# A second quad's rows loaded singly, by two engines, in a graph-attention kernel

## The chip, the cores and the metric

The kernel runs on one core of a Trainium2 chip. The metric is the device time of one execution in microseconds, from repeated runs; beside it stands one execution with the hardware profiler. Engines: PE (TensorE, matmuls; PEld is its weight loads), DVE (VectorE), ACT (ScalarE), POOL (GpSimd) and SP (SyncE). ACTq, SPq and POOLq are the queues of instructions of those engines that issue DMAs, load registers and wait.

## The reference

One layer of graph attention with 12,500 nodes, 200,000 edges sorted by target, 4 heads of 32:

```python
h = jnp.maximum(_layernorm(x, axis=-1), 0.0)
h = (node_features @ W_node.T).reshape(num_nodes, H, HD)
e = (edge_features @ W_edge.T).reshape(num_edges, H, HD)
h_src = h[src]
h_tgt = h[tgt]
att = jnp.sum(jnp.concatenate([h_src, h_tgt, e], axis=-1) * a, axis=-1)
att = jnp.where(att > 0, att, 0.2 * att)
m = jnp.maximum(jax.ops.segment_max(att, tgt, num_segments=num_nodes), 0.0)
ex = jnp.exp(att - m[tgt])
denom = jax.ops.segment_sum(ex, tgt, ...) + (num_edges - deg)[:, None] * jnp.exp(-m)
h_prime = jax.ops.segment_sum((ex / denom[tgt])[:, :, None] * h_src, tgt, ...)
x = x + h_prime
```

So each edge needs the row of its source node (h and the attention term of the source), found by an index that is known only as data.

## The kernel before, in words

Edges are cut into 392 groups of 512 (511 and a place for what is carried over); four groups are a quad, 98 quads in all, numbered from 0. A group is 4 chunks of 128 edges, so a quad has 16 chunks of 128 edges, one edge per partition.

First the node rows are made (layer norm, product with W_node) and written to a table in DRAM, 137 floats or 548 bytes a row: the four heads, counts and the source's attention terms. Then, quad by quad, POOL gathers the source rows with one indirect DMA for each chunk (128 rows, `gather`, L185) into one of eight places of the tile `ga` (quad number modulo 8). The gathers of the first quads read x itself, before the table is there.

Quads pass through three stages, which alternate in the order in which the code issues them:

- *Logits* (`all_logits`): VectorE marks each edge's target (`at`), PE multiplies edge features and target terms into `lg`, ACT copies that to `tg`. `add_sources` ends the stage: ACT waits for the quad's gathers by a semaphore that counts them, and copies the source terms out of `ga` into `U` (L798).
- *Softmax* over a super, a set of mostly four quads (`softmax`): transposes of U on PE, then VectorE and ACT in turn (`low`, scans for the running maxima, `fac`, `stack` with the exponentials, `xs`).
- *Sums* (`sums(q)`): one step for each of the quad's four groups; VectorE weighs the gathered rows and makes the one-hot `hot`, PE multiplies them into `acc`. Then the sums are passed on and divided (`passed_on` with ACT's `den_of` and VectorE's `pt`, `divide_ranges`), and ACT prepares the next quad's `hot` and `ga` columns.

While sums(q) is issued, the logits of a later quad are, and behind the logits of the last quad of a super its softmax. Supers of four start at quads 7, 11, 15 and so on, so quad 48 is the second of its super (47 to 50), and quad 42 the last of 39 to 42. Each engine takes its instructions in program order. Windows of nodes are of four kinds (`CLASSES`), and change at quads 22, 36 and 75.

One quad, the 85th (`SINGLE = 84`, counted from 0), is not gathered by POOL. Its rows are loaded one by one: behind each sums step from quad 11 on (`SINGLES_FROM`), `single_rows` issues eight (`AT_A_STEP`) DMAs of one row each on SP's queue, into a part of the tile `db` that is free by then. The row's address comes from a register: SP fetches the 128 source numbers of a chunk (`fetch_places`), VectorE scales them to byte offsets (`scale_places`), and SP loads 16 of them at a time into registers (TENSOR_LOAD). 16 chunks x 16 steps are 256 steps, the sums of quads 11 to 74. Two semaphores, one for each half, count the landings; `add_sources(84)` waits for both.

SP also issues everything else that is loaded and stored in this phase: edge features `ea`, target numbers `db`, target terms `pw`, node inputs and results.

Of the kernel before, what the change touches and what calls it, by code (L numbers as in the profile page):

```python
# [9 lines left out]
F32 = mybir.dt.float32  # L10
# [7 lines left out]
P = 128  # L18
# [21 lines left out]
QUADS = 8  # L40
# [14 lines left out]
def blocks(total, step):  # L55
    return [(i, min(step, total - i)) for i in range(0, total, step)]
# [14 lines left out]
def kernel(  # L71
# [39 lines left out]
    nc = tc.nc  # L111
    NT = -(-(N + P) // P)
    NP = NT * P
# [8 lines left out]
    table = dram.tile([NP, ROW], F32, name="table")  # L122
# [33 lines left out]
    quads = blocks(G, QG)  # L156
# [13 lines left out]
    single_came = [tc.alloc_semaphore(f"single{k}") for k in range(2)]  # L170
    landings = {}

    def gather(q, rows, width, lo, hi):

        if q == SINGLE:
            return
        g0, m = quads[q]
        ga = GA[q] = ga_all[:, q % QUADS]
        chunks = lambda i: -(-min(E - (g0 + i) * NE + 1, GE) // P)
        for i in range(lo, hi):  # L180
            if chunks(i) < J:
                nc.vector.memset(ga[:, i, chunks(i):, :], 0.0)
        order = [(i, j) for i in range(lo, hi) for j in range(chunks(i))]
        for i, j in order:
            came = nc.gpsimd.indirect_dma_start(  # L185
                out=ga[:, i, j, 0:width], out_offset=None, in_=rows,
                in_offset=bass.IndirectOffsetOnAxis(ap=srci[:, g0 + i, j:j + 1], axis=0))
# [32 lines left out]
    with tc.manual_schedule():  # L220
# [25 lines left out]
        for _ in range(AT_ONCE):  # L246
            q, i = early.pop(0)
            gather(q, x, D, i, i + 1)
# [150 lines left out]
        with tc.tile_pool(name="node", bufs=2) as node, tc.tile_pool(  # L399
# [116 lines left out]
            step, steps = 0, sum(-(-T // 3) for T in sizes) - 9  # L516
            for b, (t0, T) in enumerate(sets):
# [5 lines left out]
                row = node.tile([P, NODE_T, ROW], F32, name="row")  # L523
# [24 lines left out]
    with tc.tile_pool(name="work", bufs=2) as work, \  # L548
# [86 lines left out]
        def fetch(q):  # L635
            if q not in EA:
                due["features"] += fetch_features(q)
            fetch_windows(q)
            if q not in GATHERED:
                GATHERED.add(q)  # L640
                gather(q, table, ROW, raws(q), quads[q][1])

        def fetch_rows(s):
            g0, m = groups(s)
            dr = DR[s] = turned.tile([SBG * H, NE + 2], I32, name="dr", bufs=2)
            if finer(s) > 1:
# [8 lines left out]
        n_own = QG * J * ROW  # L655
        GA[SINGLE] = own[:, QG * GE // 2:QG * GE // 2 + n_own].bitcast(F32).rearrange(
            "p (g j r) -> p g j r", g=QG, j=J)
        places = [own[0:1, QG * GE // 2 + n_own + k * P:QG * GE // 2 + n_own + (k + 1) * P]
                  for k in range(2)]
        single = {"step": 0, "landings": 0}  # L660
        steps = -(-P // AT_A_STEP)

        def fetch_places(n):

            if n >= QG * J:
                return
            g, j = quads[SINGLE][0] + n // J, n % J
            at = ((g // 2 * J + j) * 2 + g % 2) * P
            nc.sync.dma_start(places[n % 2], src[at:at + P].unsqueeze(0))

        def scale_places(n):

            if n < QG * J:
                nc.vector.tensor_scalar(places[n % 2], places[n % 2], float(4 * ROW), None,
                                        op0=OP.mult)

        def single_rows():

            if not single["step"]:
                fetch_places(0)  # L680
                scale_places(0)
            n, at = divmod(single["step"], steps)
            if n >= QG * J:
                return
            single["step"] += 1
            if not at:
                fetch_places(n + 1)
            if at == steps // 2:
                scale_places(n + 1)
            lo = at * AT_A_STEP  # L690
            if at % 2 == 0:
                single["values"] = nc.values_load_multi_w_load_instructions(
                    places[n % 2][:, lo:lo + 2 * AT_A_STEP], engines=[mybir.EngineType.SP],
                    min_val=0, max_val=(NP - 1) * 4 * ROW,
                    skip_runtime_bounds_check_because="a node's row")[1]
            for p in range(lo, lo + AT_A_STEP):
                came = nc.sync.dma_start(
                    as_bytes(GA[SINGLE][p:p + 1, n // J, n % J, :]),
                    rows_at(table, single["values"][p - at // 2 * 2 * AT_A_STEP], 4 * ROW, 1))
                came.then_inc(single_came[2 * n // (QG * J)], 16)  # L700
                tc.no_tile_sem_insts.add(came.ins.name)
                tc.add_to_no_dep_group(f"rows{SINGLE}", came.ins)
                single["landings"] += 16

        def open_logits(q):
            if q == supers[of_quad[q]][0]:
# [47 lines left out]
        def keep_logits(q):  # L754

            pair, half, full, n = place_of(q)
            if full and q in LG:
                tg = turned.tile([PAIR * KH, GE], F32, name="tg")
                TG[of_quad[q]] = tg, n, pair
                nc.scalar.copy(tg[:n], LG.pop(q)[:n])  # L760
# [18 lines left out]
        def add_sources(q):  # L779

            s = of_quad[q]
            g0, m = quads[q]
            s0, sm = groups(s)
            keep_logits(q)
            if s not in U:
                U[s] = turned.tile([P, J, SBG * H], F32, name="U", bufs=2)
            f = finer(s)
            u = U[s][:, 0:J // f, 0:sm * H * f].rearrange("p c (h w) -> p w c h", h=H)[
                :, (g0 - s0) * f:(g0 - s0 + m) * f]
            if q == SINGLE:  # L790
                assert single["landings"] == 16 * P * QG * J
                for came in single_came:
                    nc.scalar.wait_ge(came, single["landings"] // 2)
            elif q >= QUADS:
                nc.scalar.wait_ge(arrived[q % len(arrived)],
                                  sum(landings[a] for a in range(QUADS, q + 1) if a != SINGLE
                                      and a % len(arrived) == q % len(arrived)))
            taken = nc.scalar.copy(u, GA[q][:, :m].rearrange("p g (f c) r -> p (g f) c r", f=f)[  # L798
                :, :, :, R_SRC:R_SRC + H])
# [325 lines left out]
        def sums(q):  # L1125
# [36 lines left out]
            for i in range(m):  # L1162
# [36 lines left out]
                if q >= SINGLES_FROM:  # L1199
                    single_rows()  # L1200
# [291 lines left out]
        def flush():  # L1492

            if "logits" in state:
                add_sources(state.pop("logits"))
# [441 lines left out]
```

## Time and profile before

| | us |
|---|---|
| median of 3 runs (lowest to highest) | 1971.07 (1969.68 to 1973.94) |
| profiled execution | 1973.07 |
| its span | 1971.2 |
| busy: POOL, DVE, PE, ACT | 1477.5, 1193.8, 1134.6, 318.1 |
| POOL's gathers from the table, first and last start | 93.6, 1944.0 |
| SP's single rows, first and last start | 327.8, 1601.7 |
| granted TensorE clock, mean | 0.739 of full speed |

The span runs from the first to the last instruction of the profiled execution; the rest of its time lies around it. "Busy" leaves out what queues do: an ACT or SP that issues DMAs or loads registers counts as idle. "Idle before" in a row is the time in which that engine did nothing just before the instruction, with the one that ended it.

### The profile page before, as it was taken

The page shows a single profiled execution, that of the slowest core. Times are in us where ns is not written, and L with a number is a line of the kernel's source. Part 1 is how long each engine was busy: PE and PEld are TensorE (multiplying, and loading weights), DVE is VectorE, ACT ScalarE, POOL GpSimd, SP SyncE. Part 2 cuts the span into 40 slices and gives each one's busy share as a digit, 9 for nine tenths or more (in the row PEclk, how much of TensorE's full clock was granted, in tenths as well). Part 3 has the DMA queues.
Part 4 walks back from the last instruction along what each step waited for, and adds up shares of the span by engine and source line. Part 5 has one row for each costly group of instructions (what it writes and reads, how often), then busy time and mean ns, then how long its engine had stood idle before and what let it go on. Part 6 is the DMA issues. An engine that isn't in the chain of part 4 may idle for free.

```text
span 1971.2 us, 23138 instructions
## 1 busy us (share of the span) xinstructions
PE 1134.6 (58%) x5116; PEld 771.6 (39%) x5116; DVE 1193.8 (61%) x2631; ACT 318.1 (16%) x1077; POOL 1477.5 (75%) x1569
## 2 busy tenths in 40 slices
PE   6666676454555554646556555555464755555565
PEld 4544444333333342434334333344242433334344
DVE  8676887365464663746546546466374663767576
ACT  6664111001010010100000101001011011212122
POOL 7777777777777777777777777777777777777775
PEclk9788788676776766767767677777676766877678
DMA  7754754434444444444444444444444444544442
GB/s 257 209 134 100 177 135 107 106 93 107 103 106 107 102 113 102 117 101 118 104 119 103 114 108 113 110 112 110 113 109 99 105 122 109 128 114 116 98 107 56
DMA packets 171399, 229.87 MB, mean 117 GB/s; under 512 B 62636, under 2 KB 104542, under 8 KB 171255
## 3 DMA queue, kind: packets, MB, share of 16 engines
q0 software_dynamic: 49600, 108.49, 24.5%
q1 hardware_dynamic: 119952, 117.28, 21.0%
q10 hardware_dynamic: 1702, 2.59, 0.4%
q14 instruction: 104, 0.84, 0.1%
q8 instruction: 41, 0.67, 0.1%
HBM read 210.75 MB, written 17.43 MB: 116 GB/s over the span
## 4 chain that ended last, share of the span: by engine, by line
POOL 29%; DVE 27%; PE 15%; issue 13%; DMA 9%; ACT 5%; SPq 2%; ACTq 0%; POOLq 0%; DVEq 0%
POOL ga L185 29%; DMA ga<-table,srci 6%; PE acc L1186 6%; DVE at L717 4%; PE t_ps L855 2%; PE lg L747 2%; DVE ga L1112 2%; DVE t_ps L869 1%; DVE t_ps L868 1%; DVE t_ps L935 1%; DVE t_ps L932 1%; PE lg L750 1%; DVE pt L1019 1%; DVE hot L1095 1%; PE ex_ps L950 1%
## 5 line engine op out<-in xcount | busy, mean ns | idle before, releaser
L185 POOL DMA_INDIRECT ga<-table,srci x1478 | 1399.8, 947 | 451.8 <-issue 408.9
L1186 PE MATMUL acc<-ga,hot 128*113 128x137 f32 (+1 forms) x2904 | 536.3, 344 | 83.9 <-DVE hot L1095 43.4
L1186 PEld LDWEIGHTS acc<-ga,hot 128*113 128x113 f32 (+1 forms) x2904 | 476.5, 214 | 183.8 <-issue 78.9
L1019 DVE SCALAR_TENSOR_TENSOR pt<-pt,spare,acc 1x133 f32<-1x133 f32 x113 | 38.3, 339 | 484.4 <-ACT den_of L1013 483.0
L750 PE MATMUL lg<-at,pw 112*96 112x512 bf16 (+2 forms) x392 | 155.8, 434 | 266.6 <-DVE at L717 239.4
L717 DVE TENSOR_TENSOR at<-const_ps,db 112x1024 bf16<-112x1024 f32 (+1 forms) x176 | 212.9, 1211 | 43.4 <-DMA db<-offset 41.6
L747 PE MATMUL lg<-ea,by_pair 128*96 128x512 f32 (+1 forms) x392 | 229.5, 671 | 7.1 <-ACT tg L760 7.1
L1153 DVE TENSOR_TENSOR ga<-ga,ex_ps 128x1056 f32<-128x1056 f32 x145 | 179.7, 1240 | 0.0
L855 PE MATMUL t_ps<-ident,U 128*64 128x128 f32 (+2 forms) x210 | 46.4, 391 | 216.6 <-ACT U L798 216.6
L798 ACT COPY U<-ga 128x64 f32<-128x64 f32 x97 | 28.7, 297 | 786.7 <-DMA ga<-table,srci 786.7
L1155 DVE TENSOR_TENSOR hot<-const_ps,slot 128x896 f32<-128x896 f32 (+1 forms) x147 | 144.2, 981 | 0.0
L855 PEld LDWEIGHTS t_ps<-ident,U 128*64 128x64 f32 (+2 forms) x210 | 36.5, 198 | 242.8 <-ACT U L798 239.5
L950 PE MATMUL ex_ps<-ident,stack 128*128 128x128 f32 x105 | 28.5, 423 | 173.0 <-DVE stack L942 162.3
L750 PEld LDWEIGHTS <-pw 112*96 112x96 bf16 (+2 forms) x392 | 54.3, 139 | 103.3 <-issue 97.8
L1038 PEld LDWEIGHTS acc<-pt,spare 1*2 1x2 f32 x226 | 14.0, 86 | 204.2 <-issue 195.4
L950 PEld LDWEIGHTS ex_ps<-ident,stack 128*128 128x128 f32 x105 | 18.5, 214 | 186.9 <-ACT stack L940 186.9
L1112 DVE TENSOR_TENSOR ga<-ga,ex_ps 128x528 f32<-128x528 f32 x92 | 63.6, 693 | 37.3 <-ACT xs L956 37.2
L185 POOL DMA_INDIRECT ga<-in_x_dram,srci x72 | 68.5, 951 | 23.3 <-issue 18.9
L760 ACT COPY tg<-lg 96x512 f32<-96x512 f32 (+1 forms) x51 | 29.5, 579 | 297.4 <-PE lg L750 297.4
L776 PE MATMUL t_ps<-tg,of_head 96*64 96x512 f32 (+3 forms) x96 | 72.4, 848 | 0.0
L776 PEld LDWEIGHTS t_ps<-tg,of_head 96*64 96x64 f32 (+3 forms) x96 | 11.9, 171 | 146.0 <-issue 144.0
L747 PEld LDWEIGHTS lg<-ea,by_pair 128*96 128x96 f32 (+1 forms) x392 | 63.4, 187 | 13.2 <-ACT tg L760 8.6
(222 smaller groups left out, 1306.8 us busy)
## 6 DMA issues: line engine op xcount, KB each, us to landing
ea<-in_edge_t_dram SPq DMA_DIRECT2D x196, 256.0 KB
db<-table SPq DMA_DIRECT2D x2048, 0.5 KB
ga<-table,srci POOLq DMA_INDIRECT x1478, 3.7
db<-offset SPq DMA_DIRECT2D x53, 256.0 KB
db<-in_dst_dram SPq DMA_DIRECT2D x20, 320.0 KB
db<-offset SPq DMA_DIRECT2D x35, 160.0 KB
table<-row SPq DMA_DIRECT2D x9, 616.5 KB
xt<-in_x_dram SPq DMA_DIRECT2D x9, 576.0 KB
```

The lines of the kernel that those rows point to most:

```text
L185: came = nc.gpsimd.indirect_dma_start(out=ga[:, i, j, 0:width], out_offset=None, in_=rows, in_offset=bass.IndirectOffsetOnAxis(ap=srci[:, ...
L717: nc.vector.tensor_tensor(AT[q][:span, i:i + n, :].rearrange("p g e -> p (g e)"), part_ps[:span].to_broadcast([span, n * GE]), DB[q][:span ...
L747: nc.tensor.matmul(lg, by_pair[:, begin:begin + n], ea[:, i // 2, :], start=half == 0 and i == 0, stop=False, skip_group_check=True)
L750: nc.tensor.matmul(lg, PW[q][:span, begin:begin + n], at[:span, i, :], start=False, stop=full and i == quads[q][1] - 1, skip_group_check=True)
L776: nc.tensor.matmul(TP[s][:groups(s)[1] * H], of_head[supers[s][1], p][:n], tg[:n], start=p == 0, stop=False, skip_group_check=True)
L855: nc.tensor.matmul(t_ps[:R, j * P:(j + 1) * P], u[:, j, :R], ident, start=False, stop=j == C - 1, skip_group_check=True)
L950: nc.tensor.transpose(turned_ps[:, j, :], stack[:, j * P:(j + 1) * P], ident)
L1019: nc.vector.scalar_tensor_tensor(to, row(w + at), passing[:, w + at:w + at + 1], own, op0=OP.mult, op1=OP.add)
L1112: engine.tensor_tensor(val, val, weight.unsqueeze(3).to_broadcast([P, J, H, HW]), op=OP.mult)
L1153: nc.vector.tensor_tensor(val, val, weight.unsqueeze(3).to_broadcast([P, TWO * J, H, HW]), op=OP.mult)
L1155: nc.vector.tensor_tensor(hot[:, i:i + TWO, :, 1:1 + span].rearrange("p g j c -> p (g j) c"), lane_ps[:, 0:span].unsqueeze(1).to_broadcast ...
L1186: nc.tensor.matmul(acc, hot[:, i, j, 0:1 + span], ga[:, i, j, :], start=new and j == J - 1 and not second, stop=k > 1 and i % k == k - 1 a ...
```

## The change

Quad 48 is not gathered either. `SINGLES = (48, 84)` are both loaded singly, first 48 and then 84, through the same place in `db`, 20 chunks wide instead of 16: quad 48 takes chunks 0 to 15, quad 84 chunks 4 to 19, of which 16 to 19 are filled first. Behind each sums step SP still issues eight rows, and ACT now issues eight others of the same chunk; a chunk takes 8 steps, and the 32 chunks again 256 steps. Both engines load their own 16 offsets every second step. Each quad has two semaphores, one for each engine's rows.

```diff
-SINGLE, SINGLES_FROM, AT_A_STEP = 84, 11, 8
+SINGLES, SINGLES_FROM, AT_A_STEP, BESIDE = (48, 84), 11, 8, 4
...
     def gather(q, rows, width, lo, hi):
-        if q == SINGLE:
+        if q in SINGLES:
             return
...
-        steps = -(-P // AT_A_STEP)
+        n_chunks = QG * J + BESIDE
...
+        own_rows = own[:, begin:till].bitcast(F32).rearrange("p (c r) -> p c r", r=ROW)
+        for q, lo in zip(SINGLES, (0, BESIDE)):
+            GA[q] = own_rows[:, lo:lo + QG * J, :].rearrange("p (g j) r -> p g j r", j=J)
+        singles = [(0, c, c) for c in range(QG * J)] + [
+            (1, c, BESIDE + c) for c in chain(range(QG * J - BESIDE, QG * J),
+                                              range(QG * J - BESIDE))]
+        steps = P // (2 * AT_A_STEP)
...
-            lo = at * AT_A_STEP
-            if at % 2 == 0:
-                single["values"] = nc.values_load_multi_w_load_instructions(
-                    places[n % 2][:, lo:lo + 2 * AT_A_STEP], engines=[mybir.EngineType.SP],
...
-            for p in range(lo, lo + AT_A_STEP):
-                came = nc.sync.dma_start(
...
+            for e, (engine, of) in enumerate(((nc.sync, mybir.EngineType.SP),
+                                              (nc.scalar, mybir.EngineType.Activation))):
+                lo = (at // 2 * 2 + e) * 2 * AT_A_STEP
+                if at % 2 == 0:
+                    single[e] = nc.values_load_multi_w_load_instructions(
+                        places[n % 2][:, lo:lo + 2 * AT_A_STEP], engines=[of], min_val=0,
...
+                for v in range(AT_A_STEP * (at % 2), AT_A_STEP * (at % 2 + 1)):
+                    came = engine.dma_start(as_bytes(own_rows[lo + v:lo + v + 1, to, :]),
+                                            rows_at(table, single[e][v], 4 * ROW, 1))
+                    came.then_inc(single_came[2 * k + e], 16)
...
-            if q == SINGLE:
-                for came in single_came:
-                    nc.scalar.wait_ge(came, single["landings"] // 2)
...
+            if q in SINGLES:
+                k = SINGLES.index(q)
+                for came in single_came[2 * k:2 * k + 2]:
+                    nc.scalar.wait_ge(came, single["landings"][k] // 2)
```

Where ACT's new instructions stand: first its order in a softmax, from the U of a super's last quad, before (`low` to `xs` are softmax, `den_of` belongs to the sums that are issued beside it).

```order
L798 COPY U<-ga 128x4x16
L860 ACTIVATE low<-t_ps 64x511
L1013 ACTIVATE den_of<-acc 113x8
L865 COPY low<-t_ps 64x511
L928 ACTIVATE fac<-fac 1x4
L940 ACTIVATE stack<-stack 64x511
L956 COPY xs<-ex_ps 128x4x64
```

And the same place now; TENSOR_LOAD loads 16 offsets, "x8" are eight DMAs of a row.

```order
L806 COPY U<-ga 128x4x16
L705 DMA db<-table 1x548 x8
L868 ACTIVATE low<-t_ps 64x511
L1021 ACTIVATE den_of<-acc 113x8
L700 TENSOR_LOAD db
L705 DMA db<-table 1x548 x8
L873 COPY low<-t_ps 64x511
L705 DMA db<-table 1x548 x8
L936 ACTIVATE fac<-fac 1x4
L948 ACTIVATE stack<-stack 64x511
L964 COPY xs<-ex_ps 128x4x64
```

Three bursts of eight rows and one load stand within the softmax. Next, ACT's order behind that softmax, up to the second quad after it, before:

```order
L956 COPY xs<-ex_ps 128x4x64
L1084 CAST hot<-is_last 128x16
L1123 COPY ga<-xs 128x16x5
L798 COPY U<-ga 128x4x16
L1013 ACTIVATE den_of<-acc 113x8
L1084 CAST hot<-is_last 128x16
L1123 COPY ga<-xs 128x16x5
L825 CAST t_ps<-dr 64x512
L760 COPY tg<-lg 96x512
```

And now:

```order
L964 COPY xs<-ex_ps 128x4x64
L1092 CAST hot<-is_last 128x16
L1131 COPY ga<-xs 128x16x5
L700 TENSOR_LOAD db
L705 DMA db<-table 1x548 x16
L806 COPY U<-ga 128x4x16
L1021 ACTIVATE den_of<-acc 113x8
L700 TENSOR_LOAD db
L705 DMA db<-table 1x548 x8
L1092 CAST hot<-is_last 128x16
L1131 COPY ga<-xs 128x16x5
L705 DMA db<-table 1x548 x8
```

A load and two bursts stand ahead of the U copy now, and a load with one burst between that U and the next `hot` and `ga`; the same repeats in the other quads of a super, 128 rows and 8 loads for four quads. Last, SP's order where a chunk's source numbers are fetched, before (the names in brackets are what the instruction waits for):

```order
L592 TENSOR_LOAD base_row
L669 DMA db<-in_src_dram 1x128 [waits DMAHW2_49,SP_sequencer_49]
L692 TENSOR_LOAD db [waits DVE_49]
L697 DMA db<-table 1x548 x8
L606 DMA inputs<-in_x_dram 112x512 [waits DMAHW3_49]
```

And now:

```order
L592 TENSOR_LOAD base_row
L674 DMA db<-in_src_dram 1x128 [waits DMAHW4_49,SP_sequencer_49,Activation_sequencer_49]
L700 TENSOR_LOAD db [waits DVE_49]
L705 DMA db<-table 1x548 [waits Activation_49]
L705 DMA db<-table 1x548 x7
L606 DMA inputs<-in_x_dram 112x512 [waits DMAHW5_49]
```

The fetch comes every second quad instead of every fourth, and waits for ACT's register loads too.

More of the change, by code (lines that the diff above doesn't have):

```diff
@@ L169 @@
     arrived = [tc.alloc_semaphore(f"rows{k}") for k in range(QUADS)]
-    single_came = [tc.alloc_semaphore(f"single{k}") for k in range(2)]
+    single_came = [tc.alloc_semaphore(f"single{k}") for k in range(2 * len(SINGLES))]
     landings = {}
     def gather(q, rows, width, lo, hi):
-        if q == SINGLE:
+        if q in SINGLES:
             return
@@ L654 @@
         own = db_all.rearrange("p k g e -> p (k g e)")
[L655 to L660, printed above, removed]
-        steps = -(-P // AT_A_STEP)
+        n_chunks = QG * J + BESIDE
+        begin, till = QG * GE // 2, QG * GE // 2 + n_chunks * ROW
+        own_rows = own[:, begin:till].bitcast(F32).rearrange("p (c r) -> p c r", r=ROW)
+        for q, lo in zip(SINGLES, (0, BESIDE)):
+            GA[q] = own_rows[:, lo:lo + QG * J, :].rearrange("p (g j) r -> p g j r", j=J)
+        places = [own[0:1, till + k * P:till + (k + 1) * P] for k in range(2)]
+        singles = [(0, c, c) for c in range(QG * J)] + [
+            (1, c, BESIDE + c) for c in chain(range(QG * J - BESIDE, QG * J),
+                                              range(QG * J - BESIDE))]
+        single = {"step": 0, "landings": [0, 0]}
+        steps = P // (2 * AT_A_STEP)
         def fetch_places(n):
-            if n >= QG * J:
+            if n >= len(singles):
                 return
-            g, j = quads[SINGLE][0] + n // J, n % J
+            k, c, _ = singles[n]
+            g, j = quads[SINGLES[k]][0] + c // J, c % J
             at = ((g // 2 * J + j) * 2 + g % 2) * P
@@ L671, in scale_places @@
         def scale_places(n):
-            if n < QG * J:
+            if n < len(singles):
                 nc.vector.tensor_scalar(places[n % 2], places[n % 2], float(4 * ROW), None,
@@ L682, in single_rows @@
             n, at = divmod(single["step"], steps)
-            if n >= QG * J:
+            if n >= len(singles):
                 return
@@ L789, in add_sources @@
                 :, (g0 - s0) * f:(g0 - s0 + m) * f]
-            if q == SINGLE:
-                assert single["landings"] == 16 * P * QG * J
-                for came in single_came:
-                    nc.scalar.wait_ge(came, single["landings"] // 2)
+            if q in SINGLES:
+                k = SINGLES.index(q)
+                assert single["landings"][k] == 16 * P * QG * J
+                for came in single_came[2 * k:2 * k + 2]:
+                    nc.scalar.wait_ge(came, single["landings"][k] // 2)
             elif q >= QUADS:
                 nc.scalar.wait_ge(arrived[q % len(arrived)],
-                                  sum(landings[a] for a in range(QUADS, q + 1) if a != SINGLE
+                                  sum(landings[a] for a in range(QUADS, q + 1) if a not in SINGLES
                                       and a % len(arrived) == q % len(arrived)))
```

14 lines of the change are left out of this document (6 added, 8 removed).

## The prediction

> **What bounds the kernel now.** I read the busy times first, then the gathers' line, then who waits for it.
>
> ```profile
> PE 1134.6 (58%) x5116; PEld 771.6 (39%) x5116; DVE 1193.8 (61%) x2631; ACT 318.1 (16%) x1077; POOL 1477.5 (75%) x1569
> POOL 7777777777777777777777777777777777777775
> L185 POOL DMA_INDIRECT ga<-table,srci x1478 | 1399.8, 947 | 451.8 <-issue 408.9
> ```
>
> POOL is busiest and its slices are flat: 0.947 us of gather, then (1399.8 + 451.8) / 1478 = 1.253 us from one gather to the next, the rest being issue time that waits for nothing. A quad of 16 gathers is 20.0 us. The same line asked for its waits says whether POOL is ever held up, and whom it holds up.
>
> ```profile
>   PE acc L1186: 6.7, 22
> ...
>   ACT U L798: 786.7, 77
> ...
> DMA to landing us min/median/max: 2.5/4.4/7.3
> ```
>
> The first row is POOL's largest wait with a name, 0.3 us apiece, no more than the issue gap: gathers are never held by a place that is still in use. The second is the reverse: ACT, which copies the gathered source terms into U, sat 786.7 us waiting for gathers. The third is how long a gather's rows take to land. ACT then drags VectorE along, because den_of stands behind U on ACT:
>
> ```profile
> DVE pt L1019 <- ACT den_of L1013: 483.0, 49, 14.9
> ```
>
> One group of four quads (39 to 42, then their successors) in ACT's timeline shows the rhythm; columns are start, length, instruction, idle time before it and what ended it.
>
> ```profile
> 867.90 0.30 ACT L798 COPY U<-ga 128x64 f32<-128x64 f32 x1 [12.95 <-DMA ga<-table,srci]
> 870.25 0.59 ACT L860 ACTIVATE low<-t_ps 64x511 f32<-64x511 f32 x1 [2.06 <-PE t_ps L855]
> 874.90 0.58 ACT L865 COPY low<-t_ps 64x511 f32<-64x511 f32 x1 [4.01 <-DVE t_ps L863]
> 881.04 0.20 ACT L928 ACTIVATE fac<-fac 1x4 f32<-1x4 f32 x1 [5.55 <-DVE fac L927]
> 884.26 0.63 ACT L940 ACTIVATE stack<-stack 64x511 f32<-64x511 f32 x1 [3.02 <-DVE stack L939]
> 886.21 0.37 ACT L956 COPY xs<-ex_ps 128x256 f32<-128x256 f32 x1 [1.32 <-PE ex_ps L950]
> ...
> 886.85 0.29 ACT L798 COPY U<-ga 128x64 f32<-128x64 f32 x1
> ...
> 898.15 0.58 ACT L760 COPY tg<-lg 96x512 f32<-96x512 f32 x1 [10.19 <-PE lg L750]
> 906.75 0.30 ACT L798 COPY U<-ga 128x64 f32<-128x64 f32 x1 [8.02 <-DMA ga<-table,srci]
> ...
> 926.72 0.30 ACT L798 COPY U<-ga 128x64 f32<-128x64 f32 x1 [19.32 <-DMA ga<-table,srci]
> ...
> 934.59 0.58 ACT L760 COPY tg<-lg 96x512 f32<-96x512 f32 x1 [7.23 <-PE lg L750]
> 947.18 0.30 ACT L798 COPY U<-ga 128x64 f32<-128x64 f32 x1 [12.01 <-DMA ga<-table,srci]
> ```
>
> The U copies come every 20 us, gathers' pace. The softmax of a group takes 867.90 to 886.85, almost the whole 20 us; in the three periods after it ACT waits 8, 19 and 12 us. So the pace is POOL's, and the consumers have room, least behind a softmax.
>
> **The change part by part.** *Sixteen gathers leave POOL.* 16 x 1.253 = 20.0 us, and everything behind them on POOL starts that much earlier. Gathers run to the very end:
>
> ```profile
> 1943.96 0.95 POOL L185 DMA_INDIRECT ga<-table,srci  x1 [0.30 <-issue]
> ```
>
> ```profile
> 1947.31 0.30 ACT L798 COPY U<-ga 128x64 f32<-128x64 f32 x1
> ```
>
> The last U copy follows as its rows land, and the 27 us from the last gather to the end of the span hang on it; none of that is touched. Term: -20.0 us.
>
> *SyncE* issues eight rows behind each sums step as before, in the same number of steps (64 quads x 4), so nothing is added there but 16 more fetches of places, and *VectorE* gets 16 more scalings:
>
> ```profile
> L669 SPq DMA_DIRECT2D db<-in_src_dram x16: 223/269/275, 312.9 to 1437.2; - x16
> L674 DVE TENSOR_SCALAR db<-db x16: 204/205/225, 326.2 to 1472.4; 1x128 int32<-1x128 int32 x16
> ```
>
> That is 4.3 us on SP's queue and 3.3 us on VectorE over 1,280 us, hidden by VectorE's wait for den_of: nothing. Each fetch now also waits until ACT has loaded its last places of the chunk before. ACT does that two sums steps, half a quad or 10 us, earlier in program order, and ACT's delay worked out below is 7 us: no wait. Were ACT later than that, SP's prefetches of features and weights two quads ahead would stand behind it, and 20 us of prefetch distance cover them.
>
> *ScalarE* gets 2048 row loads and 128 loads of 16 values into registers, none of which the trace has on ACT. The nearest rows are SP's for the same transfer and the same load:
>
> ```profile
> 904.30 2.51 SPq L697 DMA_DIRECT2D db<-table  x8
> L697 SPq DMA_DIRECT2D db<-table x2048: 224/228/469, 327.8 to 1601.7; - x187
> L692 SPq TENSOR_LOAD <-db x128: 971/1167/1210, 326.5 to 1593.6; - x128
> ```
>
> Eight rows take 2.51 us, 0.315 us each with the move of the address; a load takes 1.17 us. Upper bound of the pitch: ACT's only transfers in a row, at the start, of 128 partitions each, come 0.44 and 0.47 us apart:
>
> ```profile
> 0.76 0.41 ACTq L264 DMA_DIRECT2D wn<-in_w_node_dram  x1
> 0.76 0.42 SPq L222 DMA_DIRECT2D srci<-in_src_by_edge_dram  x1
> 1.20 0.45 ACTq L266 DMA_DIRECT2D we<-in_w_edge_dram  x1
> 1.23 1.88 SPq L462 DMA_DIRECT2D xt<-in_x_dram  x4
> 1.67 0.45 ACTq L268 DMA_DIRECT2D ab<-in_a_cols_dram  x1
> ```
>
> SP's four of that size there come 0.47 apart too, so ACT issues as SP does, and I take 0.315, the row of the same shape. Below it there is nothing: SP's fastest is 0.224 without the move. Per quad ACT then issues for 32 x 0.315 + 2 x 1.17 = 12.4 us. Where does that go?
>
> In the softmax period three bursts of eight and one load fall into ACT's idle times of 2.06, 4.01 and 5.55 us: the first delays low from 870.25 to about 870.8, 0.5 us; the others end before VectorE's max and fac. Then a load and two bursts (6.2 us) stand between ga's copy and the next U: that U goes from 886.85 to about 893.5, den_of with it. From xs (with hot and ga, 886.9) to the U at 947.18 there are 60.3 us, in which ACT must now issue the remaining 104 rows (32.8 us) and 7 loads (8.2 us). Its own work there is under the whole group's:
>
> ```profile
> 880.00:960.00 80.00, 44.05 (x192) 29.32 (x192) 46.17 (x91) 6.57 (x24) 60.49 (x65) 0.69 0.45 110
> ```
>
> 6.57 us of ACT per 80 us; the six softmax rows above are 2.67 of them, which leaves 3.9, and I take 4.5 with the gaps. 60.3 - 32.8 - 8.2 - 4.5 - 0.5 = 14.3 us remain, so ACT is 7 us late behind a softmax, 2 us at the second U, on time at the third: the 20 us pace holds. Term: 0.
>
> *Quad 48's U waits for its two counters, long full* (its rows are issued by sums(42)), so the consumers get two quads within one period and must make up 20 us. The trace has one such place, quad 84, loaded singly already:
>
> ```profile
> 1696.36 0.30 ACT L798 COPY U<-db 128x64 f32<-128x64 f32 x1
> ...
> 1708.00 0.30 ACT L798 COPY U<-ga 128x64 f32<-128x64 f32 x1 [2.82 <-DMA ga<-table,srci]
> ...
> 1727.41 0.30 ACT L798 COPY U<-ga 128x64 f32<-128x64 f32 x1 [14.32 <-DMA ga<-table,srci]
> ```
>
> By the next quad ACT waits for gathers again. At quad 48, with 14.3 us to spare in each group of four, it takes about two groups. Meanwhile POOL must not run out of places. Quad 39 was gathered from 867.90 - 60 - 22.5 = 785 on (three quads earlier, and 20.0 + 2.5 us from a quad's first gather to its landing), its place is wanted 160 us later, at 945, and its sums are over by the U of 906.75: 38 us of room. Past the gap of quad 48 a place is wanted 20 us sooner, which leaves 18 us; the consumers' 7 us fit. Term: 0.
>
> Sum: -20.0 us. The profiled run took 1973.07 us for a span of 1971.2, so 1.9 lie outside it, and it is 2.0 over the median of 1971.07: span 1951.2, median 1951.
>
> **The rivals.** *The two queues get in each other's way (slower).* Both bursts stand behind the same sums step. If each of ACT's rows waited out one of SP's (0.228 us), the pitch is 0.543, a group takes 104 x 0.228 = 23.7 us more, 9.4 beyond the spare 14.3, 150 us over 16 groups (quads 11 to 74). POOL has 18 us of room before it stalls: 1951 + 132 = 2083. It starts to cost at a pitch of 0.463 and eats the whole gain at 0.475. Against it: in the rows at 0.76 both queues start together and take 0.41 and 0.42, no more than the later ones. For it: no burst beside a burst is in the trace. The Trainium skill, Perfetto Trace Analysis, section "DMA Instruction — HWDGE (DVE, Sync)", says that the block which generates descriptors is shared by two sequencers and that the wait for its lock lies inside an instruction's profiled time. By that rule the sum would go the way of this rival; the equal rows at 0.76 don't bear it out.
>
> *ACT issues somewhat slower, a part of the gain is lost.* At the upper bound of 0.47 a group needs 16.1 - 14.3 = 1.8 us more, 29 over 16 groups, 11 beyond the room: 1962.
>
> *No change.* If the consumers set the pace once POOL is ahead, the end stays at 1971. For it: the shares of the chain, where VectorE and PE together exceed POOL. Against it: the 786.7 us, which after quad 84 still hold waits of 14 us.
>
> **How the numbers follow.** As worked out, 1951, with 1948 to 1955 for phases at the end: 0.80. Partial gain, 1962: 0.07. No change, 1971: 0.05. Slower, 2083: 0.08. Repeats of this kernel tell some 0.2% (4 us) from no change. Faster 0.87, same 0.05, slower 0.08. The range goes from 1946 to the bound of the pitch, 1962.
>
> **What would show it.** Right: 1462 gathers from the table, still 1.25 us apart, the last at about 1924; ACT's bursts of eight in 2.5 us; the U of quad 48 with no wait; ACT's wait for gathers down from 787 to about 370 us; POOL still without waits for places. Wrong: rows on ACT over 0.46 us apart, SP's over 0.35, POOL waiting for acc or ga for whole microseconds between 1000 and 1600, or U copies more than 20 us apart throughout.

## The result, and the profile after

The changed kernel takes 1952.67 us (median of 4 runs, 1952.23 to 1953.0), the kernel before, run beside it on the same chip, 1970.77 (4 runs). The ratio is 0.9904 with a 95% interval of 0.9892 to 0.9917: 19 us less by the ratio (16 to 21), 18.1 by the medians. The profiled execution took 1952.23 us for a span of 1950.3; that of before had been 2.0 us over its median, so the two spans differ by 20.9. Of the runs below, seven fell on occasions when the kernel before itself took some 2,630 us instead of 1,971; each is compared with the kernel before of its own occasion only.

The page of the changed kernel, the lines that answer to the first ones of before (busy times, POOL's 40 slices, the gathers):

```profile
PE 1132.7 (58%) x5116; PEld 769.2 (39%) x5116; DVE 1200.9 (62%) x2647; ACT 324.2 (17%) x1077; POOL 1460.4 (75%) x1553
...
POOL 7777777777777777777777777777777777777775
...
L185 POOL DMA_INDIRECT ga<-table,srci x1462 | 1382.8, 946 | 447.1 <-issue 409.8
```

Sixteen gathers fewer, the same pace: (1382.8 + 447.1) / 1462 = 1.252 us, and POOL's slices are as flat as before. Gathers and the gaps ahead of them add up to 1829.9 us, where before they were 1399.8 + 451.8 = 1851.6. The same line asked for what it waits for, and for who waits for it:

```profile
L185 POOL DMA_INDIRECT ga<-table,srci x1462: 940/944/1416, 93.7 to 1922.0; - x183
...
  PE acc L1194: 7.6, 25
...
  ACT U L806: 422.2, 50
```

The last gather starts at 1922.0 instead of 1944.0. POOL still waits for places only 0.3 us at a time (7.6 us in 25 waits; 6.7 in 22 before). ACT's wait for gathers has gone from 786.7 to 422.2 us, and a part of what is left is time in which its queue issues rows. Two more waits that changed much, in the list of the whole program (us in total, times, longest):

```profile
DVE pt L1027 <- ACT den_of L1021: 253.2, 47, 15.9
DVE at L724 <- DMA db<-offset: 219.8, 36, 11.6
```

VectorE waits 230 us less for den_of (483.0 before), and has a new wait, for the target numbers that SP loads (`db<-offset`). That one was not foreseen; an experiment below takes most of it away. PE now waits 100.0 us for ACT's `tg`, where it was 7.1. And the chain of work that ended last, which before went through POOL's gathers for 29% of the span and through SP's queue for 2%, now reads:

```profile
POOL ga L185 20%; ACTq L705 6%; SPq L705 5%; DMA ga<-table,srci 4%; DMA db<-offset 3%; PE acc L1194 3%; DVE at L724 3%; SPq L606 2%; DVE ga L1161 2%; DVE t_ps L877 1%; DVE t_ps L876 1%; DVE hot L1163 1%; DVE t_ps L943 1%; DVE t_ps L940 1%; SPq L700 1%
```

Row loads on ACT and SP stand in it for 11% of the span. That alone doesn't show that they cost time; the runs that leave out half of the rows, below, ask that.

The single rows, by engine, and then ACT's loads into registers (ns, least, median and greatest):

```profile
L705 SPq DMA_DIRECT2D db<-table x2048: 224/228/394, 327.4 to 1592.2; - x187
...
L705 ACTq DMA_DIRECT2D db<-table x2048: 227/235/601, 327.5 to 1575.2; - x187
```

```profile
L700 ACTq TENSOR_LOAD <-db x128: 1173/1242/1387, 326.1 to 1568.2; - x128
```

One group of four quads in ACT's timeline, the one that the prediction worked out (start, length, instruction, idle time before; time in which ACTq issues counts as idle):

```profile
866.08 0.30 ACT L806 COPY U<-ga 128x64 f32<-128x64 f32 x1 [8.12 <-DMA ga<-table,srci]
866.15 2.51 ACTq L705 DMA_DIRECT2D db<-table  x8
...
884.61 0.37 ACT L964 COPY xs<-ex_ps 128x256 f32<-128x256 f32 x1 [1.32 <-PE ex_ps L958]
...
885.02 0.33 ACT L1131 COPY ga<-xs 128x80 f32<-128x80 f32 x1
886.35 5.44 ACTq L705 DMA_DIRECT2D db<-table  x16
891.83 0.30 ACT L806 COPY U<-ga 128x64 f32<-128x64 f32 x1 [6.48 <-issue]
...
906.45 0.30 ACT L806 COPY U<-ga 128x64 f32<-128x64 f32 x1 [0.32 <-DMA ga<-table,srci]
...
911.26 9.06 ACTq L705 DMA_DIRECT2D db<-table  x23
926.11 0.30 ACT L806 COPY U<-ga 128x64 f32<-128x64 f32 x1 [14.84 <-DMA ga<-table,srci]
...
946.51 0.30 ACT L806 COPY U<-ga 128x64 f32<-128x64 f32 x1 [8.65 <-DMA ga<-table,srci]
```

Behind the softmax the U at 891.83 follows the row loads, 25.75 us after the one before it; the next three are back at gathers' pace, and the group takes 946.51 - 866.08 = 80.4 us, 64 gathers. ACT's real waits in it are 0.3, then 926.11 - 920.32 = 5.8 (issuing ends at 911.26 + 9.06), then 8.65: 14.8 us to spare. Quad 48, in the same view:

```profile
987.10 0.30 ACT L806 COPY U<-db 128x64 f32<-128x64 f32 x1
...
1000.33 0.30 ACT L806 COPY U<-ga 128x64 f32<-128x64 f32 x1 [9.05 <-issue]
...
1012.25 0.30 ACT L806 COPY U<-ga 128x64 f32<-128x64 f32 x1
...
1039.17 0.30 ACT L806 COPY U<-ga 128x64 f32<-128x64 f32 x1 [6.42 <-issue]
```

```profile
1067.17 0.30 ACT L806 COPY U<-ga 128x64 f32<-128x64 f32 x1 [9.46 <-DMA ga<-table,srci]
```

The U of 48 (out of `db`) has no wait. From there to 1039 ACT is the later one (its U copies wait for issuing, not for gathers), and the U at 1067.17, quad 53's, waits for gathers again; in the kernel before, that one stood here:

```profile
1086.86 0.30 ACT L798 COPY U<-ga 128x64 f32<-128x64 f32 x1 [19.45 <-DMA ga<-table,srci]
```

So 19.7 us are in hand five quads after 48, and they are there at the end: the last U copy is at 1926.48 (1947.31 before).

```profile
1926.48 0.29 ACT L806 COPY U<-ga 128x64 f32<-128x64 f32 x1
```

SP has less room than ACT, and the prediction didn't ask how much. From 989.09 to 1458.42, 24 quads, it issues a load of target numbers every 19.56 us, and in that stretch its queue waits for others only 12.1 us in all. With eight rows a step SP is thus nearly full, less than 0.5 us a quad under the gathers' 20.0. It can't get ahead by 20 us at once past quad 48, and most of VectorE's new wait for its loads lies there: 159.2 of the 219.8 us, between 1000 and 1500.

### The profile page after: what moved, and what is told of

The parts are those of the page before. It is cut to its first block, busy times and chain, and to the rows that moved or that the text cites. A ratio compares the mean times of both kernels' runs of the same rounds, so it can differ in the third digit from the quotient of the medians.

```text
span 1950.3 us, 27408 instructions
## 1 busy us (share of the span) xinstructions
PE 1132.7 (58%) x5116; PEld 769.2 (39%) x5116; DVE 1200.9 (62%) x2647; ACT 324.2 (17%) x1077; POOL 1460.4 (75%) x1553
## 4 chain that ended last, share of the span: by engine, by line
POOL 20%; DVE 19%; issue 12%; SPq 9%; DMA 8%; PE 7%; ACTq 7%; ACT 2%; POOLq 0%; DVEq 0%
POOL ga L185 20%; ACTq L705 6%; SPq L705 5%; DMA ga<-table,srci 4%; DMA db<-offset 3%; PE acc L1194 3%; DVE at L724 3%; SPq L606 2%; DVE ga L1161 2%; DVE t_ps L877 1%; DVE t_ps L876 1%; DVE hot L1163 1%; DVE t_ps L943 1%; DVE t_ps L940 1%; SPq L700 1%
## 5 line engine op out<-in xcount | busy, mean ns | idle before, releaser
L185 POOL DMA_INDIRECT ga<-table,srci x1462 | 1382.8, 946 | 447.1 <-issue 409.8
L1194 PE MATMUL acc<-ga,hot 128*113 128x137 f32 (+1 forms) x2872 | 517.8, 338 | 83.4 <-DVE hot L1103 51.8
L1194 PEld LDWEIGHTS acc<-ga,hot 128*113 128x113 f32 (+1 forms) x2872 | 459.2, 209 | 179.8 <-issue 89.1
L724 DVE TENSOR_TENSOR at<-const_ps,db 112x1024 bf16<-112x1024 f32 (+1 forms) x176 | 213.3, 1213 | 219.8 <-DMA db<-offset 219.8
L754 PE MATMUL lg<-ea,by_pair 128*96 128x512 f32 (+1 forms) x392 | 254.4, 737 | 100.0 <-ACT tg L767 100.0
L1027 DVE SCALAR_TENSOR_TENSOR pt<-pt,spare,acc 1x133 f32<-1x133 f32 x113 | 38.3, 339 | 256.2 <-ACT den_of L1021 253.2
L806 ACT COPY U<-ga 128x64 f32<-128x64 f32 x96 | 28.4, 298 | 551.2 <-DMA ga<-table,srci 422.2
L754 PEld LDWEIGHTS lg<-ea,by_pair 128*96 128x96 f32 (+1 forms) x392 | 69.2, 205 | 109.7 <-ACT tg L767 105.2
L783 PE MATMUL t_ps<-tg,of_head 96*64 96x512 f32 (+3 forms) x96 | 61.3, 726 | 41.7 <-ACT tg L767 41.7
L991 PE MATMUL acc<-ga,hot 128*81 128x137 f32 x168 | 40.4, 329 | 25.3 <-ACT ga L999 20.7
```

The lines of the kernel that those rows point to most:

```text
L185: came = nc.gpsimd.indirect_dma_start(out=ga[:, i, j, 0:width], out_offset=None, in_=rows, in_offset=bass.IndirectOffsetOnAxis(ap=srci[:, ...
L724: nc.vector.tensor_tensor(AT[q][:span, i:i + n, :].rearrange("p g e -> p (g e)"), part_ps[:span].to_broadcast([span, n * GE]), DB[q][:span ...
L754: nc.tensor.matmul(lg, by_pair[:, begin:begin + n], ea[:, i // 2, :], start=half == 0 and i == 0, stop=False, skip_group_check=True)
L783: nc.tensor.matmul(TP[s][:groups(s)[1] * H], of_head[supers[s][1], p][:n], tg[:n], start=p == 0, stop=False, skip_group_check=True)
L1194: nc.tensor.matmul(acc, hot[:, i, j, 0:1 + span], ga[:, i, j, :], start=new and j == J - 1 and not second, stop=k > 1 and i % k == k - 1 a ...
```

## Experiments

The theory is the prediction's: POOL's gathers set the pace, each costs 1.25 us, and what the single rows add fits into idle time, ACT's most narrowly. Against it stand two rivals: that the two queues of rows cost time of their own, so that the gain is larger without them, and that the consumers set the pace, so that fewer gathers no longer help. The kernel before took 1970.86 us beside the split of 4 and 12 rows, and 1971.46 beside the four other runs that come first, on one chip; the last seven have a part of their own.

### No quad loaded singly

```diff
-SINGLE, SINGLES_FROM, AT_A_STEP = 84, 11, 8
+SINGLE, SINGLES_FROM, AT_A_STEP = -1, 999, 8
```

Made from the kernel before: all 98 quads are gathered, and no row is loaded singly.

> The kernel before without single rows: all 98 quads are gathered, SP issues no rows. Where the kernel before takes 1971 (theory A, POOL sets the pace): 1991, 20 more. Where it takes about 2630 (three chips so far; in the traces the rows of a burst on SP are 0.60 us apart instead of 0.32, a quad takes 26.5 us, and VectorE waits over 750 us for SP's target numbers): theory Q says that SP's bursts set the pace there. Without them about 23.5 us a quad in the 64 quads, 190 less, and one quad more: 2460, ratio 0.94 (0.91 to 0.97). Rival (the chips are slow everywhere, POOL sets the pace as before): 1.01.

Measured: 1992.81 us, ratio 1.0103 (1.0086 to 1.012), 20.3 us over before by the ratio (17 to 24).

```profile
ACT U L798 <- DMA ga<-table,srci: 813.5, 79, 19.5
```

ACT waits for gathers 813.5 us here, 786.7 with one quad loaded singly, by SP alone, and 422.2 with two, half of them by ACT. Taking one quad's gathers from POOL was worth about 20 us before this change too, with SP's rows in place of them. The rival by which consumers set the pace does not give that. The expectation's second half, a theory Q for occasions on which the kernel before takes about 2630 us, wasn't tested by this run, nor by the three below that name it.

### The rows of one engine alone

```diff
-                for v in range(AT_A_STEP * (at % 2), AT_A_STEP * (at % 2 + 1)):
+                for v in range(AT_A_STEP * (at % 2), AT_A_STEP * (at % 2 + 1)) if e == 1 else ():
```

Made from the changed kernel: SP's rows are left out, and ACT's issued as before; the other kernel has `e == 0`, with ACT's rows left out. The loads into registers stay, each U waits for the one counter that is left, and VectorE clears the place once, in 2.3 us. Half of the rows of quads 48 and 84 are missing from the results.

> The changed kernel with SP's rows left out: of quads 48 and 84 only ACT's half is loaded, 8 rows a step on ACT, none on SP (SP still loads the offsets; the place is cleared once). Theory A on a chip like the first: 1952. Theory Q on a slow chip: SP is free, ACT's 15.5 us a quad are under the pace, about 24 us a quad: ratio 0.93 (0.90 to 0.97). Rival R (on a slow chip it is ACT's rows that made the changed kernel 1.076): 1.05 or more.

> The changed kernel with ACT's rows left out: half of quads 48 and 84 loaded, 8 rows a step on SP, none on ACT (ACT still loads the offsets). Theory A on a chip like the first: 1952. On a slow chip: as the kernel before without the 16 gathers (0.994 and 0.998 there), some 2.4 us of register loads a quad on ACT: 0.995 to 1.02; what is missing to 1.076 is what ACT's rows cost there.

Measured: 1954.49 us with ACT's rows alone (ratio 0.9912, 0.9895 to 0.9928), 1954.74 with SP's alone (0.9913, 0.9896 to 0.9929). On the same chip a kernel with all of the changed kernel's rows, shown below (target numbers loaded sooner), took 1954.14: leaving out half of the rows, on either queue, gives no time back. The rows' own durations, ACT alone and then SP alone:

```profile
L706 ACTq DMA_DIRECT2D db<-table x2048: 227/235/497, 329.6 to 1579.7; - x187
```

```profile
L706 SPq DMA_DIRECT2D db<-table x2048: 224/228/339, 331.5 to 1591.9; - x187
```

Medians of 235 and 228 ns, the same as with both. That the bursts do stand beside each other with both shows in SP's timeline, next to ACT's burst at 866.15 (2.51 us, above), and the same burst of ACT with SP's rows left out takes no less:

```profile
866.88 2.53 SPq L705 DMA_DIRECT2D db<-table  x8
```

```profile
869.57 2.51 ACTq L706 DMA_DIRECT2D db<-table  x8
```

The two queues do not slow each other here. With ACT's rows gone, ACT waits for gathers almost as before the change:

```profile
ACT U L807 <- DMA ga<-table,srci: 742.6, 72, 21.0
```

742.6 against 422.2 us: 320 us of ACT's issuing lie in what was this wait, and the time does not show them. With SP's rows gone, VectorE's wait for the target numbers is 5.8 us, and the one for den_of is back:

```profile
DVE pt L1028 <- ACT den_of L1022: 466.7, 64, 15.5
```

So the new wait comes with SP's rows, and without it VectorE waits as long elsewhere.

### More rows on ACT: where its room ends

```diff
+SHARES = (4, 12)
...
-                lo = (at // 2 * 2 + e) * 2 * AT_A_STEP
+                each = SHARES[e]
+                lo = at // 2 * 4 * AT_A_STEP + e * 2 * SHARES[0]
...
-                for v in range(AT_A_STEP * (at % 2), AT_A_STEP * (at % 2 + 1)):
+                for v in range(each * (at % 2), each * (at % 2 + 1)):
```

SP issues four of a step's sixteen rows and ACT twelve. Rows, landings and gathers are the same in number.

> The split of 4 rows on SP and 12 on ACT once more, for a chip on which the kernel before takes 1971. Theory A with the room read from the trace after (14.8 us in a group of four quads, 0.34 us a row): 52 more rows outside the softmax 17.7 us, longer loads 2, longer bursts within the softmax 3: 8 us too much a group, 128 over 16 groups, 18 covered by POOL's room: 2060 (1990 to 2080), and POOL then waits for places. Rival E (the room is larger, or VectorE's and PE's waits give way): under 1960. On a chip that takes about 2630 for the kernel before: 1.06, as there.

Measured: 2057.29 us (2054.71 to 2058.92), ratio 1.043 (1.0412 to 1.0447); 104.6 over the changed kernel. POOL's slices, then the chain that ended last, then POOL's wait for places:

```profile
POOL 7777777777777777775566766667676765777775
...
ACTq L707 35%; ACTq L702 4%; POOL ga L186 4%; PE acc L1196 2%; PE t_ps L785 2%; PE t_ps L865 2%; DVE at L726 2%; DVE t_ps L945 2%; DVE t_ps L942 1%; DVE t_ps L879 1%; DVE t_ps L878 1%; PE ex_ps L960 1%; DVE ga L1122 1%; PE lg L756 1%; DVE hot L1105 1%
```

```profile
  PE acc L1196: 101.0, 46
```

POOL is flat up to slice 18 and then stalls for places (101.0 us, where it was 7.6), and the chain now runs through ACT's rows, 35% of the span. The gathers' line, and the U copies of a group (quads 39 to 43), from the first behind a softmax to the first behind the next:

```profile
L186 POOL DMA_INDIRECT ga<-table,srci x1462: 938/944/1402, 93.4 to 2027.6; - x183
...
864.97 0.30 ACT L808 COPY U<-ga 128x64 f32<-128x64 f32 x1 [9.75 <-issue]
...
885.53 0.30 ACT L808 COPY U<-ga 128x64 f32<-128x64 f32 x1
...
905.02 0.30 ACT L808 COPY U<-ga 128x64 f32<-128x64 f32 x1 [13.53 <-issue]
...
921.97 0.30 ACT L808 COPY U<-ga 128x64 f32<-128x64 f32 x1
...
945.23 7.94 ACTq L707 DMA_DIRECT2D db<-table  x24
953.22 0.30 ACT L808 COPY U<-ga 128x64 f32<-128x64 f32 x1 [9.46 <-issue]
```

None of them waits for gathers any more. The group takes 88.25 us: 64 rows more at 0.34 us (24 in 7.94 is 0.33) are 21.8, less the 14.8 that were to spare 7.0, and 88.25 - 80.4 = 7.8 are measured. So the bound that the prediction named for ACT is there, about 14.8 / 128 = 0.12 us per row away, and passing it is dear.

That the whole came out at 2057, with 2060 expected, is partly luck. The 16 groups from the U of quad 15 (335.77) to that of quad 79 (1745.58) take 88.1 us each, 8.0 more than 64 gathers, 128 in all. But quad 48 saves nothing while ACT is the later one, which costs 20 more and was left out: quad 79's U comes 155.6 us later than in the changed kernel (1589.97). And POOL's room of places hides some 50 us, not 18: its last gather is only 105.6 us later, and POOL waits for a place by more than a microsecond first at 947.72, when the U of quad 42 (921.97, against 866.08) is already 56 us behind.

### The target numbers loaded sooner

```diff
                 due["places"] += fetch_targets(q + 2)
+                if i == QG - 1:
+                    issue("places", all_of=True)
```

Made from the changed kernel: SP issues the load of `db<-offset` at the end of a quad's logits, ahead of two bursts of rows that stood before it.

> The changed kernel with SP's load of the target numbers issued at the end of a quad's logits instead of at the start of the next, ahead of two bursts of rows. Theory A on a chip like the first: 1952, no change, though VectorE's 220 us of waiting for them go. Theory Q on a slow chip: VectorE's wait of 750 us shrinks, 1.00 to 1.05 instead of 1.076. Rival (SP is simply full there, the order doesn't matter): 1.07.

Measured: 1954.14 us (0.9911, 0.9895 to 0.9928), the same as the two kernels with half of the rows, run beside it.

```profile
DVE at L724 <- DMA db<-offset: 91.1, 13, 11.5
```

129 of the 219.8 us of wait are gone, and no time with them. The new wait takes the place of an old one: with den_of (253.2) it is 473 us in the changed kernel, and before they were 483.0 and 41.6.

### Seven runs on another occasion

Here the kernel before took 2630.11 us (first four kernels), 2646.95 (the two repeated on another chip) and 2624.41 (the last). The chip of the two repeats is the one on which it took 1971.46 an hour later, so this is not a fixed property of the chip. The granted TensorE clock was 0.66 to 0.69 in these runs and 0.73 to 0.75 in all others; whether as a cause or an effect isn't shown. The first two kernels ask for the parts of the gain from its two sides, the next two for ACT's and SP's room.

The second quad's rows loaded as in the change, but quad 48 gathered too:

```diff
-        if q in SINGLES:
+        if q in SINGLES[1:]:
             return
...
+                if q in ASIDE:
+                    aside = nc.scalar.copy(u, ASIDE[q][:, :m].rearrange(
```

> The changed kernel with quad 48 gathered by POOL after all; its rows are still loaded singly by both engines (into their own place, waited for, one extra copy of 0.3 us, then not used). Theory A (the gain is POOL's 16 gathers, the 2048 rows on ACT are hidden): 1971, within 0.2% of the kernel before. Rival B (the rows on ACT cost time of their own, which the gathers overpaid): 1975 or more. Rival C (the gain comes from loading in two queues, not from the gathers): 1953.

> The changed kernel with quad 48 gathered by POOL after all, its rows loaded singly and not used. On a chip on which the kernel before takes 1971 (the first chip took 2630 for it, with queues standing still 0.7 us at a time on every engine): Theory A (the gain is POOL's 16 gathers, ACT's rows are hidden): 1971, within 0.3% of the kernel before. Rival B (ACT's rows cost time of their own): 1975 or more. On a slow chip again: 7% slower than before, as there.

Measured: 2817.31 us, ratio 1.073 (1.0636 to 1.0824); repeated, 2843.7, 1.0743 (1.0672 to 1.0815). That is far from the kernel before, on the side of rival B: there the rows do cost time of their own.

The kernel before with quad 48 neither gathered nor loaded:

```diff
+        if q in LEFT_OUT:
+            return
```

> The kernel before with quad 48 neither gathered nor loaded: its copies and sums run on what the place held, so the rows of one quad are left out, and ACT issues no rows. Theory A: 1970.8 - 20.0 = 1950.8; the changed kernel is at 1952.7, so loading costs 2 us or nothing. Rival B (issuing on ACT costs something that the changed kernel pays): below 1945.

> The kernel before with the rows of quad 48 left out altogether, neither gathered nor loaded. Theory A: 1951, with the changed kernel's 1952.7 at most 2 us from it. Rival B (issuing on ACT costs the changed kernel time): below 1945. On a slow chip again: 0.994 of before.

Measured: 2617.33 us, ratio 0.9941 (0.9904 to 0.9979); repeated, 2641.35, 0.998 (0.9948 to 1.0012). Twenty us would be 0.76%, a ratio of 0.9924: the first interval holds it, the second does not, and neither is the clear gain that was expected.

The shares 4 and 12 (the diff above), and 6 and 10:

> The changed kernel with 4 rows on SP and 12 on ACT behind each sums step instead of 8 and 8. In the trace after, ACT's row costs 0.34 us and ACT has 14.8 us to spare in a group of four quads. Theory A: 52 more rows outside the softmax take 17.7 us, longer loads some 2, longer bursts within the softmax some 3: 8 us too much a group, 128 over 16 groups, 18 of them covered by POOL's room: 1953 + 110 = 2060 (1990 to 2080). Rival D (ACT has more room than its idle time shows, since it is SP that is close to its limit): 1953 or less.

> The changed kernel with 6 rows on SP and 10 on ACT. Theory A: 26 more rows take 8.8 us, with loads and softmax some 11, under the 14.8 to spare: 1953, as the changed kernel. Rival (the changed kernel already stands at ACT's limit): over 1965.

Measured: 2786.53 us (1.0595, 1.0519 to 1.0671) and 2661.08 (1.0135, 1.0055 to 1.0216). The second was expected to cost nothing; it wasn't tried where the kernel before takes 1971 us.

The changed kernel itself once more:

> The changed kernel itself, beside the kernel before on the same chip. If the kernel before takes about 1971 here: 1952 (theory A and its measured gain of 18). If it takes about 2640, as on the two chips of the first experiments, on which queues stand still for 0.7 us at a time: theory A says that POOL no longer sets the pace there (it waited 494 us for places in the trace), so nothing of the 20 us is left, and ACT's rows cost as in the split of 6 and 10: 1.00 to 1.02 of the kernel before. Rival (the gain is there whatever sets the pace): 0.99.

Measured: 2825.08 us, ratio 1.0758 (1.0689 to 1.0826). This was a clear miss: 1.00 to 1.02 was expected, and the change, worth 1% elsewhere, costs 7.6% here. Its profile, the rows of SP (ns, as above), then the largest wait and POOL's for places:

```profile
L705 SPq MOVE db<-table x2048: 2/29/1402, 511.2 to 2381.0; - x187
L705 SPq DMA_DIRECT2D db<-table x2048: 1/228/1402, 511.3 to 2381.1; - x187
```

```profile
DVE at L724 <- DMA db<-offset: 750.5, 56, 29.2
...
POOL ga L185 <- PE acc L1194: 480.8, 57, 21.0
```

The median row is the 228 ns of the other runs, but some rows, and even some moves of an address into a register, 29 ns at the median, stand still for up to 1.4 us (394 and 38 ns were the greatest in the changed kernel's first profile). ACT's rows show the same, up to 1407 ns. In the timeline a burst of eight then takes 2.53, 4.80 or 11.27 us:

```profile
1199.70 11.27 SPq L705 DMA_DIRECT2D db<-table  x8
...
1213.57 2.53 SPq L705 DMA_DIRECT2D db<-table  x8
...
1217.40 4.80 SPq L705 DMA_DIRECT2D db<-table  x8
```

POOL waits 480.8 us for places, so there it is held by the consumers, and gathers taken from it could hardly show. That agrees with the first two kernels: the rows alone cost 7%, the gathers left out next to nothing. VectorE's wait for loads that SP issues late is the largest one, and SP was nearly full even in the changed kernel's first profile; that SP sets the pace there is argued from this, not shown. Nor is it shown why the queues stand still. The rows can't be the whole of it: in the first 100 us, ahead of any single row, this profile has 217 matmuls, the first one 317. The quad that is gathered and loaded was not tried where the kernel before takes 1971 us; there the kernels with one engine's rows left out stand for it.

## Why the prediction was right

*Sixteen gathers at 1.253 us, 20.0 us.* The pace was 1.252 and the last gather 21.9 us earlier; the two profiled spans differ by 20.9. The medians differ by 18.1, and the ratio's interval of 16 to 21 us holds the 20.0. The forecast time of 1951.0 is 1.7 under the median. With repeats of the kernel before 2 us either way it can't be told whether some 2 us are lost or not.

*SP and VectorE, nothing.* SP's rows kept their 228 ns and the sum is untouched; its list of waits has none for ACT's register loads, as forecast. But that SP has time was taken over from before and not worked out: its quads take 19.56 us against the gathers' 20.0, so this term was right by a margin that the prediction did not know. VectorE's busy time rose by 7.1 us rather than 3.3, under waits of hundreds. Not foreseen was the wait for `db<-offset`, 219.8 us against 41.6. That it costs nothing was not reasoned, but shown, by the run that took 129 us of it away and by the one without SP's rows.

*ACT's rows.* The U behind the softmax was put 25.6 us after the one before it, and came 25.75 after. 14.3 us to spare in a group were worked out, and 14.8 measured. But the agreement is luck in part, since terms in it were off and met. A row takes 0.34 us (16 in 5.44), not 0.315, and a load 1.24, not 1.17, so that 104 rows and 7 loads are 44.0 us, not 41.0. Bursts of eight took 2.5 us behind a U, as forecast, but 2.7 to 2.8 elsewhere, with SP's rows and without. Against that, the stretch from `ga`'s copy (over at 885.35) to the U at 946.51 is 61.2 us, not 60.3, and ACT's own work takes only what is left, 61.2 - 44.0 - 14.8 = 2.4 us of it, not the 5.0 allowed, since its queue issues on while the engine computes. An instance, from ACT's timeline:

```profile
896.21 0.23 ACTq L705 DMA_DIRECT2D db<-table  x1
896.22 0.32 ACT L1131 COPY ga<-xs 128x80 f32<-128x80 f32 x1
896.53 2.18 ACTq L705 DMA_DIRECT2D db<-table  x7
```

The row is issued beside the copy. The four-and-twelve split then tested the spare time itself, and the excess that it gave in a group (7.0 worked out, 7.8 measured) fits.

*Quad 48.* No wait at its U, as forecast; caught up by quad 53, five quads on, where two groups had been allowed. POOL doesn't wait for places, so its room sufficed, but the split puts that room at some 50 us instead of 18. The price of the first rival, 2083, thus rests on too small a room, and leaves out that quad 48 saves nothing where ACT is the later one.

*ACT's wait for gathers, about 370 us.* It was 422.2. Time in which the queue issues counts as idle in that number: of the 14.84 us at 926.11, 9 were issuing.

*The rival of the two queues.* Its break-even was a pitch of 0.475 us; 0.34 was measured with both queues at work, and the run without SP's rows shows the same 235 ns. The Trainium skill, Perfetto Trace Analysis, section "DMA Instruction — HWDGE (DVE, Sync)", puts the wait for the lock of a block that DVE and Sync share inside these durations. A note in that section says that which two engines issue such DMAs is up to the compiler, SP and ACT with neuronx-cc. Between SP and ACT these runs show no such wait: 228 and 235 ns with both queues at work and with one. *ACT slower (0.47, 1962)* fell by the same pitch. *No change* fell by the result, and by the kernel with all quads gathered: each quad taken from POOL gave about 20 us.

What the prediction did not hold was that its price of nothing for the queues depends on how they run on the day: on another occasion the same change was 7.6% slower, which none of its rivals covers, since each of them priced the rows at one fixed pitch.

## What to carry to other kernels

Where one engine paces a pipeline flatly, work taken from it is worth its count times its pace, if every queue that takes the work over has the time within each period: add up the issue time there, rows and register loads, against the waits that the timeline shows on that engine, less the issuing that counts as idle. Here 44 us of issuing fitted into 61; 64 more rows in a group, 22 us, did not, and cost 105. Ask the same of the queue that already did this work: SP's quads took 19.56 us against the gathers' 20.0, so gathers faster by half a microsecond a quad would probably meet SP, which no run here tried. A new wait in the list is no cost in itself: take it away once, and see whether the time moves.

## What was not expected of the hardware

SP's and ACT's queues, issuing transfers of 548 bytes at the same time, don't slow each other: 228 and 235 ns with both, 228 and 235 alone.

On some occasions SP's and ACT's queues stood still for up to 1.4 us now and then, and the same kernel took 2,617 to 2,664 us instead of 1,971, in one case on a chip that took 1,971 an hour later. The median row was unchanged at 228 ns. What stops the queues is open. The kernel with twice as many single rows lost 7.6% to its predecessor there, and the shares of the two queues, 8 and 8, 6 and 10, 4 and 12, gave ratios of 1.076, 1.014 and 1.060 (the first on another chip than the others), while 8 and 8 beat 4 and 12 by 105 us where the kernel before takes 1971.
